# Layer 0 of two tiles at a time, full-height half chunks in attention, and loads at the turn between two phases of a four-layer net

## The chip, the cores and the metric

The kernel runs on one core of a Trainium2 chip, as one launch. The metric is the device time of one execution in microseconds (us); the number of a kernel is the median over its executions. A core has a matrix engine, TensorE (PE), whose weight loads are listed apart (PEld); three engines for elementwise work, VectorE (DVE), ScalarE (ACT) and GpSimd (POOL); and SyncE (SP), which only issues DMAs here. Each engine takes its instructions in the order of the program.

## The reference

The input x has 64 batches of 64 tokens of 512 numbers, all in float32. Four layers follow, each added to its input.

```python
x = x + (x @ W0[id] + b0[id])                  # layer 0: one of 16 matrices, chosen per batch
x = x + (x @ W1.T + ((x @ A[a].T) @ Bm[a].T) * s[a])   # layer 1: one matrix, plus a rank-16 adapter per batch
x = x + attention(x)                           # layer 2, below
x = x + (w3[sub].T @ x + b3[sub][:, None])     # layer 3: over a batch's 64 tokens, one of 8 matrices
```

Layer 2 has 8 query heads and 4 groups of keys and values of 64 numbers. Queries and keys are normalised by their root mean square, scaled by a gain and rotated by their position. New keys and values go into a paged cache at positions pos..pos+63 of each batch; a query sees the 256 positions up to its own. A softmax over these, the product with the values, and a matrix Wo end the layer.

## The kernel before, in words

The 4096 tokens are 32 tiles of 128 rows, two batches to a tile. **Phase A** (0 to about 520 us) does layers 0 and 1 and the products that make q, k and v. **Phase B** (about 520 to 954 us) does attention, layer 3 and the output, a tile per step. The program is written in the order in which every engine works (a manual schedule), so a line's place in the Python text is its place in each engine's queue, SyncE's and GpSimd's too.

*Layer 0* (`layer0`, from L243). `load_next(i)` asks SyncE for the input of tile i+2 (`load_x`, L222) and the two matrices of 1 MB that its batches use (`load_w0`, L232). Four buffers `w` exist, two tiles' worth. L249 multiplies: each matmul makes the 64 rows of one batch, so two run side by side on halves of the array's columns. ScalarE copies the result to `s0` (L252; one buffer). `add_bias` (L260, GpSimd) makes x1 = x + bias. `turn0` transposes `s0` (L273) and VectorE adds it into x1 (L274). Each matmul of the program shows as two records in the trace (L249: 8 a tile, 512 records).

*Layer 1* (`layer1`, from L612) takes a group of tiles: adapter products `pxa` (L620) and their selection `xa` (L625, VectorE), 16 matmuls a tile (L635), the adapter's second product (L643), a copy and a store of x2 (L648, L649). The groups are `GROUPS = [1, 1, 2] + [4] * 7`. After layer 1 of a group, the loop at the end of phase A (from L708) goes through the tiles of the *next* group: for each, `layer0`, `load_next`, `other`, then for one tile of the group just finished `turn_x2` (L654), the product for q (L140), `turn0` of the new tile, and the product for k and v with its normalisation and rotation: `turned` (L120 to L135), in which VectorE's L133 and L134 need the gain tiles cg and sg that GpSimd makes (L110), and GpSimd makes the sum (L135).

*`other`* feeds work in small pieces between the tiles: index and window work on VectorE (`windows`, among it `hit` and `own` at L535 and L539), rotation angles, and `old`: the copy of old cache rows. Each of 68 pieces is a GpSimd gather into a buffer `st` (L155, five buffers) and a SyncE store of 512 KB into `kvd` (L161), which is issued when three later gathers have been asked for. `other` takes pieces of `old` from tile 6 on; `layer1` takes one per tile too (from tile 4).

*The turn between the phases.* The q of the last eight tiles is left for the beginning of phase B. `parts_q` is a generator of three parts: Square, sum and Sqrt; reciprocal and scale; rotation. `turn_q` (L170 to L183) transposes (L174), ScalarE copies to `qTs` (L177; two buffers), SyncE stores to `qTd` (L181). Before the first step stand the loads of q, mask (`load_mask`) of tiles 0 and 1, `wo` and q of tile 2.

*Phase B, step s.* `load_kv(s+2)` gathers keys and values (L768, GpSimd). `scores(s)`: matmuls (L841), mask and maximum on VectorE (L849), exponential on ScalarE (L853). `attend(s-1)` multiplies probabilities by values (L888), `normalise` divides (L861, L865), `last` is layer 3 of two tiles at even steps (L928), `project(s-2)` multiplies by Wo (L916) into the one PSUM bank of the pool `pyp` and adds x2 (L920), `keys(s+1)` transposes keys (L822, L828; copies L823, L829), `turn(s)` transposes probabilities (L874, L878) into `pT` (L875 on VectorE and ScalarE, L879 on ScalarE). The queries of one batch see 320 positions: two chunks of 128 rows that belong to the batch, and a *half chunk* of 64. The half chunks of the two batches of a tile share one chunk of 128 rows: rows 0 to 63 belong to the first batch, 64 to 127 to the second. `attend` treats each with its own matmuls of 64 rows:

```python
for gp in range(2):
    for b2 in range(2):
        for g in (2 * gp, 2 * gp + 1):
            product(b2, g, slice(b2 * 64, (b2 + 1) * 64), 4, G, g, False, gp == 1)
```

PSUM has eight banks: seven in a ring that all products but one take in turn, and the one of `pyp`, which `project` uses at every step and which q of tile 31 uses at step 0.

Of the kernel before, what the change touches and what calls it, by code (L numbers as in the profile page):

```python
# [22 lines left out]
KC = D // 128  # L23
# [36 lines left out]
def body(ctx: ExitStack, tc: tile.TileContext, a: dict, out: bass.AP):  # L60
# [108 lines left out]

    def turn_q(i):  # L170
        qrf = qrs.pop(i)
        pqt = bank("pqt")
        for c in range(KC):
            TE.transpose(pqt[:, c * 128 : (c + 1) * 128], qrf[:, c * 128 : (c + 1) * 128], ident)  # L174
        qT = late.tile([128, 2, 2, 2, T], F32, name="qTs", bufs=2)
        for gp in range(2):
            S.copy(  # L177
                qT[:, gp].rearrange("p b h t -> p h b t"),
                pqt[:, gp * 256 : (gp + 1) * 256].rearrange("p (h b t) -> p h b t", h=2, b=2),
            )  # L180
        nc.sync.dma_start(  # L181
            qTd[i * 128 : (i + 1) * 128, :], qT.rearrange("p g b h t -> p (g b h t)")
        )  # L183

    with ExitStack() as pa:
# [57 lines left out]
        def layer0(i, bias=True):  # L243

            p0 = bank("p0")
            for c in range(KC):
                for h in range(2):
                    hs = slice(h * T, (h + 1) * T)
                    TE.matmul(p0[hs, :], xs[i][:, c, hs], w0s[i][h][:, c, :], start=c == 0, stop=c == KC - 1)  # L249
            w0s.pop(i)  # L250
            s0 = s0s[i] = wk.tile([128, D], F32, name="s0")
            S.copy(s0, p0)  # L252
            if bias:
                add_bias(i)
# [412 lines left out]

        biasT = su.tile([128, KC, B], F32, name="biasT")
        pb = bank("pb")
        for c in range(KC):  # L670
            TE.transpose(pb[:, c * B : (c + 1) * B], brow[:, c * 128 : (c + 1) * 128], ident[:B, :B])
        S.copy(biasT.rearrange("p c b -> p (c b)"), pb[:, : KC * B])
        layer0(0)
        turn0(0)
# [21 lines left out]
        def other(i):  # L696

            next(bg, None)
            next(bg, None)

            o = (i + 2) // 8
            if 0 < o < NT // 8 and i <= 8 * o + 2:
                next(turns.setdefault(o, rotation(o)), None)
            if i > 5:
                for _ in range(2 - i % 2):
                    next(old, None)

        for g in range(NG - 1):  # L708
# [6 lines left out]
            for k in range(m):  # L715
                i0, i = tiles[g + 1][k], tiles[g][k * n // m] if (k + 1) % (m // n) == 0 else None
                layer0(i0)
                load_next(i0)
                other(i0)
# [147 lines left out]
    def turn(i):  # L867
        pr, _ = prs.pop(i)

        pT = pTs[i] = bp.tile([128, G + 1, 512], F32, name="pT")  # L870
        for g in range(G):
# [5 lines left out]
        for g in range(G):  # L877
            TE.transpose(pt[:, g * 128 : (g + 1) * 128], pr[:, g, 256:384], ident)  # L878
        S.copy(pT[:, G, :], pt)  # L879

    def attend(i):
        kv, pT = kvs.pop(i), pTs.pop(i)
        oT = oTs[i] = bp.tile([128, KC, 2, T], F32, name="oT")
        po = [bank("po") for _ in range(2)]

        def product(b2, g, rows, n, c, m, start, stop):
            gp, g2 = divmod(g, 2)
            TE.matmul(  # L888
                po[b2][g2 * 64 : (g2 + 1) * 64, gp * 128 : (gp + 1) * 128],
                kv[rows, n, (G + g) * HD : (G + g + 1) * HD], pT[rows, c, m * 128 : (m + 1) * 128],  # L890
                start=start, stop=stop,
            )

        for b2 in range(2):
            for gp in range(2):
                for c in range(2):
                    for g in (2 * gp, 2 * gp + 1):
                        n = 2 * b2 + c

                        product(b2, g, slice(0, 128), n, g, n, gp == 0 and c == 0, False)  # L900
        for gp in range(2):
            for b2 in range(2):
                for g in (2 * gp, 2 * gp + 1):
                    product(b2, g, slice(b2 * 64, (b2 + 1) * 64), 4, G, g, False, gp == 1)
        for b2 in range(2):
            V.tensor_copy(oT[:, :, b2, :], po[b2][:, :256].rearrange("p (k t) -> p k t", t=T))

# [48 lines left out]
    for i in range(2):  # L956
        load_kv(i)
        load_q(i)
        load_mask(i)
    wo = bp.tile([128, KC, D], F32, name="wo", bufs=1)  # L960
    nc.sync.dma_start(wo, a["woT"].rearrange("(c p) f -> p c f", p=128))
    load_q(2)

    parts = {}
    for i in range(NT - LATE + 1, NT - 1):
# [3 lines left out]
        if i > NT - LATE + 2:  # L969
            turn_q(i - 2)  # L970
        if i - 1 in parts:
            run(parts.pop(i - 1))
        next(parts[i])
    keys(0)
    for s in range(NT):
        if s + 2 < NT:
# [9 lines left out]
        if s:  # L986
            load_pair(s - 1)
            attend(s - 1)
        else:

            parts[NT - 1] = parts_q(NT - 1, product(NT - 1, wq, "pq", pyp), V, cs[NT - 1])
            turn_q(NT - 3)
        normalise(s, 0)
        if s == 1:
            next(parts[NT - 1])
            next(parts[NT - 1])
        normalise(s, 1)
# [4 lines left out]
        if s + 1 < NT:  # L1002
            keys(s + 1)
        if s in (3, 4):
            turn_q(NT - 5 + s)
        turn(s)
        if s in (2, 3):
            run(parts.pop(NT - 4 + s))
    i = NT - 1
# [62 lines left out]
```

## Time and profile before

| what | value |
| --- | --- |
| median of 11 executions | 956.37 us (954.7 to 959.03) |
| the profiled execution: its own time | 956.01 us |
| its span in the profile | 953.9 us |
| its mean granted clock of TensorE | 0.995 |
| weight loads busy | 508.4 us |
| HBM read and written | 190.29 and 69.50 MB |
| L888 in all | 82.1 us in 1536 records |
| L249 in all | 121.6 us in 512 records |
| L155, gathers of old cache rows | 68, about 1.0 us each on GpSimd |

The profile is of one execution. "Busy" is the time that an engine worked, and its share of the span. A row of a group of instructions names the line, engine, operation, what it writes and reads, and how many there are. In a timeline, a row begins with its start and its duration; in brackets stands how long the engine had been idle before it and what ended that. The view of waits sums these by what was waited for. Durations of pipelined matmuls overlap a little, so what one costs is read from the start of one record to that of the next.

### The profile page before, as it was taken

The numbers are of one execution on the slowest core, as the hardware profiler recorded it, in microseconds if no ns is written. First come the engines' busy times: TensorE is split into PE (matmuls) and PEld (weight loads), VectorE is DVE, ScalarE is ACT, GpSimd is POOL, SyncE is SP. The second block draws the span as 40 slices with busy tenths as digits, with TensorE's granted clock in tenths as the row PEclk, the third lists the DMA queues.
The fourth block names the chain that finished last, engine by engine and source line by source line (L and its number), as shares of the span: only waits on it lengthen the run. The fifth ranks groups of instructions, "written<-read, shape, count | busy, mean of one in ns | idle before, by whom it ended". The sixth has DMA issues, their size and how long they took to land.

```text
span 953.9 us, 17790 instructions
## 1 busy us (share of the span) xinstructions
PE 922.5 (97%) x5397; PEld 508.4 (53%) x5397; DVE 613.9 (64%) x1736; ACT 415.0 (44%) x1084; POOL 404.9 (42%) x599
## 2 busy tenths in 40 slices
PE   4999999999999999999999799999999999999998
PEld 1344444444444444444344367666777777766665
DVE  3755998888573263532315778777777777777773
ACT  0312144221342221432213376666666666666663
POOL 3333465455353453544434454344444444444400
PEclk9999999999999999999999989999999999999999
DMA  7988999999999999999984784666666666666621
GB/s 247 354 278 274 340 363 328 385 396 332 382 340 368 397 323 394 397 340 387 398 295 178 262 255 143 216 218 193 207 201 205 202 207 203 206 208 208 206 62 46
DMA packets 133344, 260.97 MB, mean 274 GB/s; under 512 B 32737, under 2 KB 41570, under 8 KB 133250
## 3 DMA queue, kind: packets, MB, share of 16 engines
q1 hardware_dynamic: 108562, 178.61, 52.1%
q0 software_dynamic: 23280, 79.84, 25.5%
q10 hardware_dynamic: 1408, 1.39, 0.5%
q8 instruction: 43, 0.70, 0.3%
q14 instruction: 51, 0.42, 0.1%
HBM read 190.29 MB, written 69.50 MB: 272 GB/s over the span
## 4 chain that ended last, share of the span: by engine, by line
PE 69%; DMA 3%; DVE 2%; SPq 1%; ACT 1%; issue 0%; POOL 0%; ACTq 0%; DVEq 0%
PE py L916 12%; PE po L888 8%; PE ps L841 8%; PE p L635 7%; PE pk L140 7%; PE ppt L874 6%; PE p L249 6%; PE pq L140 5%; PE pkt L822 2%; PE ppt L878 2%; PE pkt L828 1%; PE pz L928 1%; DMA qTd<-qTs 1%; DMA w<-in_W 1%; PE px L654 1%; PE pqt L174 1%
## 5 line engine op out<-in xcount | busy, mean ns | idle before, releaser
L768 POOL DMA_INDIRECT kv<-kvd,idxn x128 | 126.2, 986 | 194.3 <-PE po L888 151.5
L853 ACT ACTIVATE pr<-pr,mx 128x320 f32<-128x320 f32 x256 | 140.1, 549 | 23.3 <-DVE mx L849 23.3
L849 DVE CUSTOM_DVE_ANT_0 pr<-ps,mb 128x320 f32<-128x320 f32 x256 | 107.9, 486 | 27.9 <-PE ps L841 27.5
L249 PE MATMUL p<-w,xt 128*64 128x512 f32 x512 | 121.6, 607 | 0.5 <-DMA w<-in_W 0.5
L916 PE MATMUL py<-wo,oT 128*128 128x512 f32 (+1 forms) x264 | 118.3, 591 | 0.0
L140 PE MATMUL pk<-wkv,x 128*128 128x512 f32 x256 | 115.4, 595 | 1.4 <-ACT x L656 1.4
L155 POOL DMA_INDIRECT st<-in_kvc,cidx x68 | 68.4, 1006 | 104.0 <-DMA kvd<-st 96.1
L635 PE MATMUL p<-w,x 128*128 128x512 f32 x256 | 112.5, 596 | 0.0
L140 PE MATMUL pq<-wq,x 128*128 128x512 f32 x248 | 111.3, 593 | 0.0
L841 PE MATMUL ps<-kT,qT 64*128 64x320 f32 x512 | 81.9, 454 | 5.5 <-ACT kT L823 5.3
L865 DVE TENSOR_SCALAR pr<-pr,sm 128x320 f32<-128x320 f32 x256 | 85.6, 396 | 2.2
L274 DVE TENSOR_TENSOR x<-pt,x 128x512 f32<-128x512 f32 x32 | 22.0, 688 | 98.6 <-PE pt L273 91.6
L888 PE MATMUL po<-pT,kv 128*64 128x128 f32 (+1 forms) x1536 | 82.1, 278 | 0.0
L888 PEld LDWEIGHTS po<-pT,kv 128*64 128x64 f32 (+1 forms) x1536 | 68.9, 135 | 19.8 <-DVE mx L849 13.6
L916 PEld LDWEIGHTS py<-wo,oT 128*128 128x128 f32 x264 | 47.5, 189 | 59.8 <-issue 58.6
L635 PEld LDWEIGHTS p<-w,x 128*128 128x128 f32 x256 | 47.8, 190 | 58.2 <-issue 56.5
L135 POOL TENSOR_TENSOR qr<-qn,sq 128x512 f32<-128x512 f32 x25 | 31.7, 1268 | 107.6 <-DVE qn L134 107.6
L140 PEld LDWEIGHTS pk<-wkv,x 128*128 128x128 f32 x256 | 46.3, 190 | 49.7 <-issue 47.4
L249 PEld LDWEIGHTS p<-w,xt 128*64 128x64 f32 x512 | 35.2, 138 | 70.4 <-issue 67.0
L140 PEld LDWEIGHTS pq<-wq,x 128*128 128x128 f32 x248 | 44.9, 190 | 46.2 <-issue 46.2
L133 DVE TENSOR_TENSOR sq<-qn,sg 128x256 f32<-128x256 f32 (+1 forms) x128 | 40.1, 354 | 42.2 <-POOL sg L110 40.2
L123 ACT ACTIVATE ss<-ss,epst 128x4 f32<-128x4 f32 (+1 forms) x64 | 19.2, 299 | 107.4 <-DVE ss L122 107.4
(191 smaller groups left out, 1358.3 us busy)
## 6 DMA issues: line engine op xcount, KB each, us to landing
w<-in_W SPq DMA_DIRECT2D x62, 1024.0 KB
kvd<-st SPq DMA_DIRECT2D x68, 512.0 KB
xt<-in_xT SPq DMA_DIRECT2D x32, 256.0 KB
x2d<-x2n SPq DMA_DIRECT2D x32, 256.0 KB
kvd<-kvn SPq DMA_DIRECT2D x32, 256.0 KB
qTd<-qTs SPq DMA_DIRECT2D x32, 256.0 KB
qT<-qTd SPq DMA_DIRECT2D x32, 256.0 KB
x2r<-x2d SPq DMA_DIRECT2D x32, 256.0 KB
```

What stands on the lines that cost most here:

```text
L140: TE.matmul(ps, x2s[i][:, c, :], w[:, c, :], start=c == 0, stop=c == KC - 1)
L155: P.indirect_dma_start(out=st, out_offset=None, in_=a["kvc"].rearrange("(n r) d -> n (r d)", r=2), in_offset=bass.IndirectOffsetOnAxis(ap= ...
L249: TE.matmul(p0[hs, :], xs[i][:, c, hs], w0s[i][h][:, c, :], start=c == 0, stop=c == KC - 1)
L635: TE.matmul(p1[i], x1s[i][:, c, :], w1[:, c, :], start=c == 0, stop=False)
L768: P.indirect_dma_start(out=kv[:, n, :], out_offset=None, in_=kvd, in_offset=bass.IndirectOffsetOnAxis(ap=at, axis=0),)
L841: TE.matmul(ps[g2][:, :NPOS], qT[rows, gp, b2].rearrange("p h t -> p (h t)"), kT[rows, gp, b2 * NPOS : (b2 + 1) * NPOS], start=True, stop= ...
L849: V.tensor_tensor_reduce(out=p, in0=ps[g2][:, :NPOS], in1=mb[:, b2, :], scale=-1.0, scalar=3.0e38, op0=ALU.add, op1=ALU.min, accum_out=mx[ ...
L853: S.activation(p, p, AF.Exp, bias=mx[:, g, b2 : b2 + 1], scale=-1.0, accum_out=sm[:, g, b2 : b2 + 1],)
L865: V.tensor_scalar(p, p, sm[:, g, b2 : b2 + 1], None, ALU.mult)
L874: TE.transpose(pt[:, n * 128 : (n + 1) * 128], pr[:, g, at : at + 128], ident)
L888: TE.matmul(po[b2][g2 * 64 : (g2 + 1) * 64, gp * 128 : (gp + 1) * 128], kv[rows, n, (G + g) * HD : (G + g + 1) * HD], pT[rows, c, m * 128 ...
L916: TE.matmul(py[:, fs], oT[:, c].rearrange("p b t -> p (b t)"), wo[:, c, fs], start=c == 0, stop=c == KC - 1,)
```

## The change

It has five parts. (1) Layer 0 of tile 0 stands before the transposes of the bias rows, and its `add_bias` after them. (2) In groups of four tiles, layer 0 of two tiles is done in one go at every even tile, then the loads for both next tiles; `s0` gets two buffers. (3) `other` takes pieces of `old` from tile 4 on, not from tile 6. (4) In attention the half chunks are done with matmuls of all 128 rows and both batches at once (256 columns); the probabilities lie in one of two tiles `hT`, which hold zeros where a row belongs to the other batch and are cleared once, by four memsets on VectorE ahead of phase B. Results go to one PSUM bank instead of two, and one copy takes them out instead of two. The copy of the half chunks' probabilities is split in two copies of 64 rows, one on ScalarE and one on VectorE. (5) At the beginning of phase B, q and mask of tile 1 are loaded behind the first `keys`, `wo` and q of tile 2 behind the first `turn`; `qTs` of the late tiles gets four buffers; the transposes of q of tiles 30 and 31 come a step later; and the parts of q of tiles 30 and 31 are moved to other places in steps 1 to 3.

```diff
@@ -167,12 +167,12 @@
         for _ in parts:
             pass
 
-    def turn_q(i):
+    def turn_q(i, pool=late):
         qrf = qrs.pop(i)
         pqt = bank("pqt")
         for c in range(KC):
             TE.transpose(pqt[:, c * 128 : (c + 1) * 128], qrf[:, c * 128 : (c + 1) * 128], ident)
-        qT = late.tile([128, 2, 2, 2, T], F32, name="qTs", bufs=2)
+        qT = pool.tile([128, 2, 2, 2, T], F32, name="qTs", bufs=2 if pool is late else 4)
         for gp in range(2):
             S.copy(
                 qT[:, gp].rearrange("p b h t -> p h b t"),
@@ -248,7 +248,7 @@
                     hs = slice(h * T, (h + 1) * T)
                     TE.matmul(p0[hs, :], xs[i][:, c, hs], w0s[i][h][:, c, :], start=c == 0, stop=c == KC - 1)
             w0s.pop(i)
-            s0 = s0s[i] = wk.tile([128, D], F32, name="s0")
+            s0 = s0s[i] = wk.tile([128, D], F32, name="s0", bufs=2)
             S.copy(s0, p0)
             if bias:
                 add_bias(i)
@@ -666,11 +666,12 @@
         scalars()
 
         biasT = su.tile([128, KC, B], F32, name="biasT")
+        layer0(0, False)
         pb = bank("pb")
         for c in range(KC):
             TE.transpose(pb[:, c * B : (c + 1) * B], brow[:, c * 128 : (c + 1) * 128], ident[:B, :B])
         S.copy(biasT.rearrange("p c b -> p (c b)"), pb[:, : KC * B])
-        layer0(0)
+        add_bias(0)
         turn0(0)
         load_next(0)
         load_weight(wq, "wqT")
@@ -701,7 +702,7 @@
             o = (i + 2) // 8
             if 0 < o < NT // 8 and i <= 8 * o + 2:
                 next(turns.setdefault(o, rotation(o)), None)
-            if i > 5:
+            if i > 3:
                 for _ in range(2 - i % 2):
                     next(old, None)
 
@@ -714,8 +715,15 @@
             n, m = len(tiles[g]), len(tiles[g + 1])
             for k in range(m):
                 i0, i = tiles[g + 1][k], tiles[g][k * n // m] if (k + 1) % (m // n) == 0 else None
-                layer0(i0)
-                load_next(i0)
+                if m < 4:
+                    layer0(i0)
+                    load_next(i0)
+                elif k % 2 == 0:
+
+                    for i1 in (i0, i0 + 1):
+                        layer0(i1)
+                    for i1 in (i0, i0 + 1):
+                        load_next(i1)
                 other(i0)
                 if i0 % 4 == 1 and i0 // 4 + 1 < NT // 4:
                     load_a(i0 // 4 + 1)
@@ -867,7 +875,7 @@
     def turn(i):
         pr, _ = prs.pop(i)
 
-        pT = pTs[i] = bp.tile([128, G + 1, 512], F32, name="pT")
+        pT = pTs[i] = bp.tile([128, G, 512], F32, name="pT")
         for g in range(G):
             pt = bank("ppt")
             for n, at in enumerate((0, 128, 384, 512)):
@@ -876,34 +884,37 @@
         pt = bank("ppt")
         for g in range(G):
             TE.transpose(pt[:, g * 128 : (g + 1) * 128], pr[:, g, 256:384], ident)
-        S.copy(pT[:, G, :], pt)
+
+        ht = hTs[i % 2]
+        for b2, copy in enumerate((S.copy, V.tensor_copy)):
+            hs = slice(b2 * 64, (b2 + 1) * 64)
+            copy(ht[hs, :, b2, :], pt[hs].rearrange("p (g n) -> p g n", g=G))
 
     def attend(i):
         kv, pT = kvs.pop(i), pTs.pop(i)
         oT = oTs[i] = bp.tile([128, KC, 2, T], F32, name="oT")
-        po = [bank("po") for _ in range(2)]
-
-        def product(b2, g, rows, n, c, m, start, stop):
-            gp, g2 = divmod(g, 2)
-            TE.matmul(
-                po[b2][g2 * 64 : (g2 + 1) * 64, gp * 128 : (gp + 1) * 128],
-                kv[rows, n, (G + g) * HD : (G + g + 1) * HD], pT[rows, c, m * 128 : (m + 1) * 128],
-                start=start, stop=stop,
-            )
-
+
+        po = bank("po").rearrange("p (k b n) -> p k b n", k=2, b=2)
         for b2 in range(2):
             for gp in range(2):
                 for c in range(2):
-                    for g in (2 * gp, 2 * gp + 1):
-                        n = 2 * b2 + c
-
-                        product(b2, g, slice(0, 128), n, g, n, gp == 0 and c == 0, False)
+                    for g2 in range(2):
+                        g, n = 2 * gp + g2, 2 * b2 + c
+
+                        TE.matmul(
+                            po[g2 * 64 : (g2 + 1) * 64, gp, b2], kv[:, n, (G + g) * HD : (G + g + 1) * HD],
+                            pT[:, g, n * 128 : (n + 1) * 128], start=b2 == 0 and gp == 0 and c == 0, stop=False,
+                        )
         for gp in range(2):
-            for b2 in range(2):
-                for g in (2 * gp, 2 * gp + 1):
-                    product(b2, g, slice(b2 * 64, (b2 + 1) * 64), 4, G, g, False, gp == 1)
-        for b2 in range(2):
-            V.tensor_copy(oT[:, :, b2, :], po[b2][:, :256].rearrange("p (k t) -> p k t", t=T))
+            for g2 in range(2):
+                g = 2 * gp + g2
+                TE.matmul(
+                    po[g2 * 64 : (g2 + 1) * 64, gp], kv[:, 4, (G + g) * HD : (G + g + 1) * HD],
+                    hTs[i % 2][:, g], start=False, stop=gp == 1,
+                )
+        V.tensor_copy(
+            oT.rearrange("p (k h) b t -> p k b h t", k=2), po.rearrange("p k b (h t) -> p k b h t", h=2)
+        )
 
     def project(i, ring=False, parts=1):
         py, oT = bank("py") if ring else pyp.tile([128, 512], F32, name="py"), oTs.pop(i)
@@ -955,11 +966,13 @@
 
     for i in range(2):
         load_kv(i)
-        load_q(i)
-        load_mask(i)
-    wo = bp.tile([128, KC, D], F32, name="wo", bufs=1)
-    nc.sync.dma_start(wo, a["woT"].rearrange("(c p) f -> p c f", p=128))
-    load_q(2)
+    load_q(0)
+    load_mask(0)
+
+    hTs = [bp.tile([128, G, 2, 128], F32, name=f"hT{n}", bufs=1) for n in range(2)]
+    for hT in hTs:
+        for b2 in range(2):
+            V.memset(hT[(1 - b2) * 64 : (2 - b2) * 64, :, b2, :], 0.0)
 
     parts = {}
     for i in range(NT - LATE + 1, NT - 1):
@@ -967,11 +980,14 @@
         parts[i] = parts_q(i, pq, V, cs[i])
         next(parts[i])
         if i > NT - LATE + 2:
-            turn_q(i - 2)
+            turn_q(i - 2, bp)
         if i - 1 in parts:
             run(parts.pop(i - 1))
         next(parts[i])
     keys(0)
+    load_q(1)
+    load_mask(1)
+    wo = bp.tile([128, KC, D], F32, name="wo", bufs=1)
     for s in range(NT):
         if s + 2 < NT:
             if s < 2:
@@ -989,11 +1005,10 @@
         else:
 
             parts[NT - 1] = parts_q(NT - 1, product(NT - 1, wq, "pq", pyp), V, cs[NT - 1])
-            turn_q(NT - 3)
+            turn_q(NT - 3, bp)
+        if s == 2:
+            next(parts[NT - 1])
         normalise(s, 0)
-        if s == 1:
-            next(parts[NT - 1])
-            next(parts[NT - 1])
         normalise(s, 1)
         if s % 2 == 0 and s >= 4:
             last(s - 4)
@@ -1001,11 +1016,17 @@
             project(s - 2)
         if s + 1 < NT:
             keys(s + 1)
-        if s in (3, 4):
-            turn_q(NT - 5 + s)
+        if s in (4, 5):
+            turn_q(NT - 6 + s, bp)
+        elif s in (2, 3):
+
+            run(parts.pop(NT - 4 + s))
         turn(s)
-        if s in (2, 3):
-            run(parts.pop(NT - 4 + s))
+        if s == 0:
+            load_q(2)
+            nc.sync.dma_start(wo, a["woT"].rearrange("(c p) f -> p c f", p=128))
+        elif s == 1:
+            next(parts[NT - 1])
     i = NT - 1
     load_pair(i)
     add_one(i - 1)
```

## The prediction

> **What bounds the kernel now.** I read busy time first. Columns: busy microseconds, share of the span, instructions; the two rows below give 40 slices of 23.8 us, in tenths.
>
> ```profile
> PE 922.5 (97%) x5397; PEld 508.4 (53%) x5397; DVE 613.9 (64%) x1736; ACT 415.0 (44%) x1084; POOL 404.9 (42%) x599
> ...
> PE   4999999999999999999999799999999999999998
> ...
> PEclk9999999999999999999999989999999999999999
> ```
>
> TensorE (PE) works 97% of the span. The weak slices are the first, and the 23rd (the transition to attention), where the clock row also dips. So time comes from TensorE's work, its few waits, and the clock. The view of TensorE's waits lists all the waits there are (total, times, longest):
>
> ```profile
> PE pb L671 <- DMA brow<-in_b,idcol: 11.1, 1, 11.1
> PE ps L841 <- ACT kT L823: 5.3, 1, 5.3
> PE pt L273 <- ACT s L252: 3.7, 7, 0.8
> PE pxa L620 <- DVE x L274: 2.8, 3, 1.0
> PE ppt L874 <- DVE pr L865: 2.3, 2, 2.1
> ```
>
> The profiled execution's own time is 956.01 us (span 953.9, so 2.1 around it); the median shown is 956.37. I sum against 956.0. Within 0.2%, 1.9 us, is about what a measurement of this kernel can't tell from no change.
>
> A table of busy time by stretch gives the second fact:
>
> ```profile
> 85.00:250.00 165.00, 161.06 (x634) 71.09 (x632) 143.38 (x251) 42.87 (x101) 90.11 (x126) 1.00 0.95 346
> 250.00:520.00 270.00, 268.63 (x1031) 119.60 (x1028) 110.40 (x277) 82.87 (x186) 122.58 (x224) 1.00 0.95 350
> ```
>
> The third pair is VectorE (DVE): 143 of 165 us in the first stretch, 110 of 270 in the second. In VectorE's timeline up to 233 us I found no idle but answers of 0.4 to 0.6 us from ScalarE (ACT) and GpSimd (POOL), while TensorE waits there for VectorE's x1 (1.02 at 103.14, 0.92 at 233.73). Both are at the limit there; what TensorE alone saves before 233 is taken back at the next such wait.
>
> **Start: 0 (-0.4 to +0.4).** Layer 0 of tile 0 now goes ahead of the bias transposes. TensorE waits 11.11 us for brow, and L249 runs 11.70 to 17.36, its last W0 pieces landing at 15.0. In front it could begin at 10.2, yet ends about 16.0 because of those pieces. Then pb, a copy, the bias copy, GpSimd's adds (1.65 us, now after layer 0 and not beside it), and L274 at about 18.85; it stood at 18.84.
>
> **Pairs of layer 0: -3.5 by themselves.** In single records, a matmul of L249 starts 0.429 us after the one before it; the first after a full-array one needs 0.573, and leaving for a transpose needs 0.261 where 0.109 is usual. So one block costs 0.144+0.152 = 0.296 in changes of tile shape, and a pair saves one of its two. Seven groups of four hold two pairs each. The last four groups, after 250 us, win 4x2x0.296 = 2.4, and tiles 29 to 31 lose their wait of pt for the s0 copy (0.37 each): 1.1. Of the first three groups only the first pair, ahead of VectorE's full stretch, could keep its saving (0.9: one change of shape and most of the 0.77 that pt waits at tile 4), and only if VectorE is not delayed behind it. The bounds for 3.5 are 2.4 (the waits of pt move elsewhere) and 4.4.
>
> **Three gathers moved forward: +6.7 (0 to +11).** The old cache copies start two tiles earlier. GpSimd now:
>
> ```profile
> 98.27 1.36 POOL L110 TENSOR_TENSOR cg<-gain,cos 128x64 f32<-128x64 f32 x1
> 99.59 0.31 POOL L110 TENSOR_TENSOR sg<-gsw,sin 128x64 f32<-128x64 f32 x1
> ...
> 118.36 0.94 POOL L155 DMA_INDIRECT st<-in_kvc,cidx x1 [5.62 <-DMA kvd<-st]
> ```
>
> Five st buffers exist, so the sixth gather waits for the first store of one to land: here 5.62 us at 118.36, while VectorE is occupied with `hit` work that doesn't need GpSimd. After the change the sixth gather stands in tile 7's slot, ahead of cg/sg. Its store is issued by SyncE (SP) behind the loads of w(8) and w(9), two tiles now in one go: 4.5 MB with xt. In the trace these go out at 91.6 to 95.8 and land from 97.5 to 110.8, so the store lands at about 110; then gather and gains, and VectorE's next row can start at about 111.8:
>
> ```profile
> 102.40 0.68 DVE L274 TENSOR_TENSOR x<-pt,x 128x512 f32<-128x512 f32 x1
> ...
> 105.08 0.76 DVE L133 TENSOR_TENSOR sq<-qn,sg 128x256 f32<-128x256 f32 x2
> ```
>
> 111.8-105.1 = 6.7 us of VectorE's full chain, behind which stand `xa`, the adapter work and the x1 adds that TensorE needs up to 233. Nothing is lost if the store overtakes the loads; 11 if the next odd slot also waits (the row at 118.36 was 5.6). I take 6.7, being the landing that the trace shows. Phase A: +6.7-3.5 = **+3.2**; without the stall -0.9-3.5 = -4.4.
>
> **Transition: -6.1 (-9 to -2).** ScalarE's qTs copy waits for a qTd store that stands behind q1, mask1, wo and q2 in the queue, and delays the kT copy, for which TensorE waits; a half clock follows:
>
> ```profile
> 543.21 0.65 ACT L177 COPY qTs<-pqt 128x256 f32<-128x256 f32 x2 [5.88 <-DMA qTd<-qTs]
> ```
> ```profile
> 546.38 4.64 PE L841 MATMUL ps<-kT,qT 64*128 64x320 f32 x16 [5.33 <-ACT kT L823]
> ...
> 568.40 1.93 PE L874 MATMUL ppt<-ident,pr 128*128 128x128 f32 x8 [2.05 <-DVE pr L865]
> ```
>
> With four qTs buffers and the loads behind, the wait is about 1.1: -4.2. The sixteen score matmuls need 2.4 in place of 4.64: -2.1 with the overlap. At step 1 tile 31's rotation leaves the normalises, so 2.05+0.24 go, and 3.4 us at half clock behind them: -4.0. At step 2 project(0) waits about 1.75 for the PSUM bank that q of tile 31 still holds, and parts of tile 30 stand ahead of the pT copies (0.65): +2.4, with a half clock behind a 1.75 wait, priced by its nearest row (2.05): +1.7. Steps 3 and 4: L841 took 3.31 there against 2.42; half comes back: -1.0. Four zero memsets on VectorE wait for the last kvn store (issued 520.3, landed 523.4; its SBUF region is reused) and then hold the reduction at 521.2, so tile 25's q turn: no memset of that size is in the trace; 0.06 each (a 128x1 memset, L405) to 0.69 (a 128x512 copy), taken 0.35, +1.1 at TensorE (0 to 2.5). q2 and wo, moved behind turn(0), go out at about 552 and are read at about 564 and 570; in the trace they landed 11.0 and 9.8 us after issue with 2 MB ahead of them, so they cost nothing, and a late one costs what it is late. Sum -6.1.
>
> The clock row, 0.83 for 540 to 560, shows half clock behind 5.33 and behind 2.05 us. [...]
>
> **Half chunks: +10.6 (8.5 to 12.2).** One step of attention:
>
> ```profile
> 646.51 2.42 PE L841 MATMUL ps<-kT,qT 64*128 64x320 f32 x16
> 648.86 2.56 PE L888 MATMUL po<-pT,kv 128*64 128x128 f32 x48
> 651.25 1.04 PE L928 MATMUL pz<-x,w 64*64 64x512 f32 x8
> 652.21 3.70 PE L916 MATMUL py<-wo,oT 128*128 128x512 f32 x8
> ```
>
> Of the 48 records, 16 are half chunks of 64 rows. In single records four of these start within 7 ns and a quad takes 0.109: four quads and one change of shape (0.141) make 0.598. The new form has 4 calls with 128 rows and 256 columns, eight records, of which only two run side by side: four pairs at twice 0.109 = 0.216 make 0.864 and no change of shape. +0.266 a step, 32 steps: +8.5. In the 15 even steps L928 (64x64) followed such a half chunk without a change; it now follows 128x64 records: 15x0.141 = +2.1. VectorE per step gains one pT half copy (0.69) and loses one of the two oT copies; its idle of 0.92 in front of L849 hides that. With that cover gone: 0.05 a step, 1.6 more.
>
> [...]
>
> **Sum: 956.0 + 0 + 3.2 - 6.1 + 10.6 = 963.7 us.**
>
> **Rivals.**
> - Forecast, chance 0.50, own range 959 to 969.
> - *The gather is hidden* (0.25): its store lands before 105, or VectorE has other work first. Phase A is -4.4: 956.0-4.4-6.1+10.6 = 956.1, own range 953.5 to 959. For: VectorE kept working through 118.36 now. Against: L133 waits for sg, 37 times in the trace.
> - *Transition wins in full* (0.12): faster. No half clock at step 2, no memset delay, qTs free: -9, which decides once the gather is hidden as well and the transition is under -8.1. 956.1-2.9 = 953.2, and 951.1 if L928 pays no change of shape. Against: project(0)'s bank.
> - *Loads starve* (0.13): two tiles of W0 asked for at once leave 4.5 MB in front of every store and gather; later odd slots wait too, at 11 in place of 6.7, with the transition at -2: 963.7+4.3+4.1 = 972.1. DMA share 0.95 speaks for it; TensorE's slack after 250 (VectorE 41% busy) against.
> - That the change doesn't do what it says isn't seen: instruction order on each engine moves as told.
>
> Range 952.5 to 970.0: leaves out the most of the fourth case and a half of the third. Faster by over 0.2% (under 954.5): 0.12 plus 0.05 of the second; same: 0.13 of the second and 0.02 of the forecast; slower: 0.48+0.07+0.13.
>
> **What would show it.** L888's group per step 2.83 us instead of 2.56, L928's 1.18, L906 once per step. A GpSimd gather at about 110 with a wait on kvd<-st of over 5 us, and L133 near 112. PE at the x1 wait of 233 some 6 us later. The wait for kT about 1 us. I am wrong if a step of attention grows by less than 0.2 us, if the sixth gather doesn't wait, or if the clock dip at 545 stays.

## The result, and the profile after

The changed kernel takes 1029.68 us (median of 8, 1024.8 to 1031.18) against 956.02 for the kernel before (median of 31); the ratio is 1.0761, 95% interval 1.0746 to 1.0776. The forecast was 963.7 with a range up to 970.0: the direction was right, the size wrong by a factor of ten. The profiled execution has a span of 1030.8, 76.9 more than the 953.9 of before. In some sets of runs the kernel before takes 975 to 980 us and in others 956 to 958, so a run below is compared by its ratio to the kernel before in the same set, and lengths in attention are read from sets at 956 to 958 alone.

The page of the changed kernel, busy time and the rows of TensorE (40 slices of 25.8 us):

```profile
PE 969.3 (94%) x5141; PEld 526.3 (51%) x5141; DVE 633.5 (61%) x1740; ACT 414.4 (40%) x1084; POOL 398.9 (39%) x599
...
PE   5999988997998989979989999999999999999998
...
PEclk9999989998999999999999999999999999999999
```

The weak slices are no longer two; they are spread over the whole of phase A, which is now the first 23 slices, and in two of them, the sixth and the tenth, the clock row dips to 8 tenths. TensorE is busy 46.8 us longer and idle 30.1 us longer. Its waits (total, times, longest), then those of all engines that matter:

```profile
PE pk L140 <- ACT x L656: 20.6, 13, 3.9
PE p L249 <- DMA w<-in_W: 17.3, 10, 8.6
PE pt L273 <- ACT s L252: 7.0, 6, 1.7
PE pxa L620 <- DVE x L274: 3.7, 3, 1.9
```
```profile
POOL st L155 <- DMA kvd<-st: 175.0, 23, 16.4
...
DVE sq L133 <- POOL sg L110: 121.5, 44, 14.3
```

The last two rows are the story. The same two in the kernel before:

```profile
POOL st L155 <- DMA kvd<-st: 96.1, 30, 7.2
...
DVE sq L133 <- POOL sg L110: 40.2, 37, 4.5
```

GpSimd waits 175.0 us for stores of old cache rows (96.1 before), and VectorE waits 121.5 us for the gain tiles that stand behind on GpSimd (40.2 before). The first of the changed kernel's long waits, on GpSimd and then on VectorE:

```profile
113.25 0.93 POOL L155 DMA_INDIRECT st<-in_kvc,cidx  x1 [16.37 <-DMA kvd<-st]
114.19 0.34 POOL L110 TENSOR_TENSOR cg<-gain,cos 128x64 f32<-128x64 f32 x1
```
```profile
114.83 0.76 DVE L133 TENSOR_TENSOR sq<-qn,sg 128x256 f32<-128x256 f32 x2 [9.37 <-POOL sg L110]
```

This is the sixth gather where the forecast had put it, 9.37 us of VectorE's time and not 6.7. The forecast counted it once. GpSimd's wait returns in the odd places, from the next group on (10.04 at 156.54, 9.21 at 187.93, 10.49 at 230.18), and VectorE waits 5.42, 5.10 and 7.54 us behind these three.

To say where the time went I read five marks off each trace: the end of the last group's layer 1, the first transposes of keys (L822 in the kernel before), the first `attend`, the sixth, and the length of a step as the mean of the 20 steps behind the sixth `attend`.

| trace | layer 1 ends | to keys(0) | to first attend | to the sixth | a step |
| --- | --- | --- | --- | --- | --- |
| before | 496.3 | 43.5 | 21.2 | 63.5 | 12.184 |
| after | 554.2 | 47.2 | 15.5 | 64.5 | 12.962 |
| difference | +57.9 | +3.7 | -5.7 | +1.0 | +0.778 |

From the sixth `attend` to the end of the span the changed kernel takes 20.0 us more. 57.9+3.7-5.7+1.0+20.0 = 76.9, the whole difference of the spans. So 57.9 us is phase A (61.6 up to keys(0), the figure in some of the expectations below), and about 24 (0.778 a step) is attention. Phase A loses all the way: layer 1 of tiles 12 to 15 ends at 274.3, 24.5 us late, and the other 33.4 us come after that.

### The profile page after: what moved, and what is told of

Read it like the earlier page. It is cut to its first block, busy times and chain, and to the rows that moved or that the text cites. A ratio compares the mean times of both kernels' runs of the same rounds, so it can differ in the third digit from the quotient of the medians.

```text
span 1030.8 us, 17263 instructions
## 1 busy us (share of the span) xinstructions
PE 969.3 (94%) x5141; PEld 526.3 (51%) x5141; DVE 633.5 (61%) x1740; ACT 414.4 (40%) x1084; POOL 398.9 (39%) x599
## 4 chain that ended last, share of the span: by engine, by line
PE 64%; DMA 8%; DVE 5%; ACT 2%; POOL 2%; issue 1%; SPq 0%; ACTq 0%; DVEq 0%; POOLq 0%
PE py L927 11%; PE ps L849 8%; DMA kvd<-st 7%; PE p L635 7%; PE pk L140 6%; PE po L904 6%; PE ppt L882 5%; PE pq L140 4%; PE p L249 4%; PE po L911 3%; PE pkt L830 2%; PE pz L939 1%; DMA w<-in_W 1%; PE pkt L836 1%; PE ppt L886 1%
## 5 line engine op out<-in xcount | busy, mean ns | idle before, releaser
L140 PE MATMUL pk<-wkv,x 128*128 128x512 f32 x256 | 132.8, 669 | 20.7 <-ACT x L656 20.6
L249 PE MATMUL p<-w,xt 128*64 128x512 f32 x512 | 126.8, 606 | 17.3 <-DMA w<-in_W 17.3
L155 POOL DMA_INDIRECT st<-in_kvc,cidx x68 | 66.6, 979 | 185.5 <-DMA kvd<-st 175.0
L133 DVE TENSOR_TENSOR sq<-qn,sg 128x256 f32<-128x256 f32 (+1 forms) x128 | 40.1, 355 | 123.0 <-POOL sg L110 121.5
L140 PEld LDWEIGHTS pk<-wkv,x 128*128 128x128 f32 x256 | 52.1, 213 | 82.0 <-issue 57.6
L849 PE MATMUL ps<-kT,qT 64*128 64x320 f32 x512 | 92.1, 449 | 1.5 <-issue 1.2
L249 PEld LDWEIGHTS p<-w,xt 128*64 128x64 f32 x512 | 37.8, 138 | 99.1 <-issue 76.8
L849 PEld LDWEIGHTS ps<-kT,qT 64*128 64x128 f32 x512 | 55.5, 186 | 27.4 <-issue 6.6
L904 PE MATMUL po<-pT,kv 128*64 128x128 f32 x1024 | 63.0, 276 | 0.0
```

What stands on the lines that cost most here:

```text
L140: TE.matmul(ps, x2s[i][:, c, :], w[:, c, :], start=c == 0, stop=c == KC - 1)
L155: P.indirect_dma_start(out=st, out_offset=None, in_=a["kvc"].rearrange("(n r) d -> n (r d)", r=2), in_offset=bass.IndirectOffsetOnAxis(ap= ...
L849: TE.matmul(ps[g2][:, :NPOS], qT[rows, gp, b2].rearrange("p h t -> p (h t)"), kT[rows, gp, b2 * NPOS : (b2 + 1) * NPOS], start=True, stop= ...
L904: TE.matmul(po[g2 * 64 : (g2 + 1) * 64, gp, b2], kv[:, n, (G + g) * HD : (G + g + 1) * HD], pT[:, g, n * 128 : (n + 1) * 128], start=b2 == ...
```

## The experiments

The marks of phase A are alike in all sets: layer 1 of the last group ends at 496.3 to 498.4 in seven traces of kernels that leave phase A's loop alone.

**Which part of the change costs phase A?**

b2_pair: the kernel before with the pairs alone.

```diff
-                layer0(i0)
-                load_next(i0)
+                if m < 4:
+                    layer0(i0)
+                    load_next(i0)
+                elif k % 2 == 0:
+                    for i1 in (i0, i0 + 1):
+                        layer0(i1)
+                    for i1 in (i0, i0 + 1):
+                        load_next(i1)
```

> The kernel before with part 2 alone: layer 0 of two tiles in one go, both loads behind, two s0 buffers; old cache copies from tile 6, attention and the turn between the phases as before. Theory A (pairing sets off GpSimd's waits for kvd and the chain behind them, from the second group on): about 50 us slower than before, 1000 to 1012, GpSimd's wait of st for kvd 140 us or more. Rival C (the pair needs the early start of the copies to do harm): 952 to 962.

Ratio 1.047 (1.0427 to 1.0513); layer 1 ends at 546.4, 50.1 us late; GpSimd waits 161.6 us for kvd. The pairs alone do most of the harm.

b3_i3: the early start of the old copies alone (`if i > 5` to `if i > 3`).

> The kernel before with part 3 alone: old cache copies from tile 4. My forecast's mechanism without pairs: the sixth gather, in tile 7's place, waits for the first store with the loads of one tile and not of two ahead of it, and holds the gains. The markers of c2_nopair, against those of c3_trans, give 5.4 us up to the end of the last layer 1. Expected: 958 to 963, ratio 1.003 to 1.007. Rival (hidden, as the 5.62 us wait of before was): within 0.2%.

Ratio 1.0018 (1.0005 to 1.0031). GpSimd's sixth gather does wait, 8.36 us at 105.76, but VectorE only 2.14 for the gains behind it, and layer 1 ends at 499.7, 3.4 later than in the kernel before. Part 3 alone is worth 0.1 to 0.3%, less than I expected.

c2_nopair: the changed kernel with layer 0 tile by tile; all else of the change stays.

> The changed kernel without part 2: layer 0 tile by tile, one s0 buffer; the rest of the change, the early start of the copies included, stays. Theory A: phase A is that of before within 3 us, so what is left is attention (0.778 us a step measured in the changed kernel, 32 steps, +24.5) and the turn between the phases (about -5): 956+24.5-5 = 975, range 970 to 980. Rival C (the early start by itself costs): over 985.

Layer 1 ends at 503.1, so 51.1 of the 57.9 us go with the pairs. The ratio, 1.0403 (1.0368 to 1.0438), is far over the 975 expected: this set was one of those at 979.5, where attention's new form costs more (b4_half below). In phase A 6.8 us stay, where theory A allowed 3; for the total the run tells nothing.

a2_i5: the changed kernel with old copies from tile 6.

> The changed kernel, with the old cache copies starting at tile 6 again and not at tile 4. Theory A (loads of a pair in front of the stores, at every pair): the earlier start only sets where the first wait falls; 5 to 20 us come back, 1010 to 1025. Rival C (the earlier start is the cause, as my forecast had it with one wait of 6.7 us): phase A comes back to that of before, 965 to 975.

1023.5 to 1026.4 in two runs, ratio 1.072 (1.0686 to 1.0755); GpSimd still waits 161.7 us, and layer 1 ends at 545.3, 8.9 us earlier. Rival C falls: the early start is not the cause of most of it.

**How do the pairs cost it?**

a1_spread: the pair of matmuls stays, the loads go out one tile at a time.

```diff
-                    for i1 in (i0, i0 + 1):
-                        load_next(i1)
+                if m >= 4:
+                    load_next(i0)
```

> The changed kernel, but the loads for the next two tiles no longer go out together behind a pair of layer 0: those for the first stand behind the pair, those for the second behind the next tile's place, as before the change. The matmuls stay in pairs. Theory A (the stores of old cache rows stand behind 4.5 MB of W0 at every pair; the third gather of each pair waits for one of them on GpSimd and holds the gain tiles, so VectorE, k and v, and SyncE's queue): nearly all of the 61.6 us that phase A lost comes back; time 965 to 975, GpSimd's wait of st for kvd under 110 us (it was 175.0). Rival B (two layer 0 blocks back to back starve for W0 or wait for s0): less than 20 us come back, 1010 or more.

A miss, with the time that rival B forecast: 1024.4 us, ratio 1.0715 (1.0684 to 1.0746). GpSimd's wait fell as theory A says, to 63.1 us, and VectorE's for the gains to 20.1, but layer 1 still ends at 547.7. TensorE's rows show why:

```profile
148.90 1.04 PE L249 MATMUL p<-w,xt 128*64 128x512 f32 x2 [3.11 <-DMA w<-in_W]
152.90 5.84 PE L249 MATMUL p<-w,xt 128*64 128x512 f32 x14 [2.96 <-DMA w<-in_W]
```

The second tile's matrices are now asked for a place later and behind the stores of k, v and q on SyncE, while the pair needs them a place earlier. TensorE waits 36.5 us for W0 (17.3 in the changed kernel), twice in a pair, and then runs 14 records in 5.84 us instead of 3.65. One wait was exchanged for another.

a5_ahead2: each store of old rows issued one gather earlier (`copies(kvd[:OLD], op, 3)` to `2`).

> The changed kernel, with each store of old cache rows issued one gather earlier (two gathers are asked ahead, not three), all else the same. The store on which the third gather of a pair waits then stands ahead of the pair's loads in SyncE's queue. Theory A: GpSimd's wait for kvd falls under 100 us and at least 40 of the 61.6 us come back, 965 to 990. Rival B (layer 0 pairs starve): no more than 15 us come back. Against both: SyncE may now wait for gathers to land, which would show as its own wait of L161 for st, over 60 us (25.4 now).

988.43 us, ratio 1.0338 (1.0303 to 1.0374): 41 us come back with one digit. GpSimd waits 48.2 us for kvd, layer 1 ends at 508.1. SyncE's order shows why. In the changed kernel the gather at 156.54 waits for a store that was issued at 142.12, behind the pair's loads of W0 (132.9 to 137.7); here the store for the same gather, the 13th, goes out at 122.91, ahead of those loads (129.1 to 133.3), and the gather does not wait for it.

e2_gainsfirst: the gain tiles of a place made ahead of its gathers.

```diff
+                gq = gains(0, asked[-1], late, P) if asked and i is not None else None
+                gk = gains(1, i, wk, P) if i is not None else None
                 other(i0)
```

> The changed kernel, with the gain tiles cg and sg of a place made on GpSimd ahead of the gathers; the gathers and stores stay where they are. If the gain tiles are the link between the waiting gather and VectorE: VectorE's wait of L133 for sg falls from 121.5 to under 50 us, and layer 1 of the last group ends at 515 to 535 (554.2), since the sums qr and kvn are still behind the gather. If these sums alone are the link: it ends at 545 or later, with another wait in L133's place.

993.81 us, ratio 1.0383 (1.0361 to 1.0405); layer 1 ends at 513.9, 40.3 us earlier. Here are the waits of this kernel:

```profile
POOL st L155 <- DMA kvd<-st: 145.9, 22, 15.4
```
```profile
DVE sq L133 <- POOL sg L110: 1.7, 1, 1.7
```

GpSimd waits nearly as long as ever, and it costs little, since nothing that VectorE needs at once stands behind it: a5_ahead2 and d1_gatherlast (below), each with 98 us less of this wait, end layer 1 only 5.8 and 1.5 us earlier. That is the clearest of the runs: not the wait, but what is queued behind the waiting instruction. d2_best and e1_x2early look for the cause of the 17.6 us that are left against the kernel before.

d1_gatherlast: the changed kernel with the gathers at the end of a place.

```diff
-            if i > 3:
-                for _ in range(2 - i % 2):
-                    next(old, None)
...
+                if i0 > 3:
+                    for _ in range(2 - i0 % 2):
+                        next(old, None)
```

> The changed kernel, with the gathers of old cache rows (and the stores that go with them) at the end of a tile's place in the program instead of its beginning, behind the gains and rotations of q, k and v; how many and in which tile's place is unchanged. Theory A, first form (the harm is done by what stands behind a waiting gather on GpSimd: gain tiles and sums, so VectorE, k and v): GpSimd goes on waiting for kvd, 100 us or more in all, but the layer 1 of the last group ends within 15 us of before's 496.3 (554.2 in the changed kernel), time 975 to 990. Theory A, second form (the harm is done by SyncE's queue, loads late behind stores): it ends at 530 or later, time 1005 or more.

Layer 1 ends at 512.4, 16.1 later than before: near the first form's 15 and far from the second's 530. But GpSimd's own wait fell too, to 47.7 us, where the first form had 100 or more, so this run alone would not tell the link. Its time, ratio 1.0574 (1.0546 to 1.0603), is of a set at 976 and holds attention's new form.

d2_best: parts 1, 2 and 5 in the kernel before, gathers last.

> The kernel before with parts 1, 2 and 5 of the change (layer 0 of tile 0 first, pairs of layer 0 with both loads behind, the turn between the phases), the old copies from tile 6 as before, but their gathers at the end of a tile's place; attention as before. If pairs are harmless once the gathers stand last: 945 to 955, ratio to before 0.988 to 0.999. If pairs do harm in another way: 965 or more.

Ratio 1.0126 (1.0089 to 1.0163), layer 1 ends at 514.1. The hope that pairs are harmless once the gathers stand last falls: 17.8 us of phase A stay.

e1_x2early: d2_best, with the x2 transposes and copies of both tiles in the even place.

```diff
-                if i is not None:
+                if i is not None and (m < 4 or n < 4):
                     turn_x2(i)
+                elif i is not None and k % 2 == 0:
+                    for i1 in (i, i + 1):
+                        turn_x2(i1)
```

> The kernel of the earlier run d2_best (parts 1, 2 and 5, gathers last, attention of before), and in pairs the x2 transposes and ScalarE's copies of both tiles stand in the even tile's place. With gathers last, pairs still end layer 1 of the last group at 514.1 where 496.5 is usual; TensorE waits 10.1 us for the x2 copy (L656) ahead of k and v, with half clock behind. Theory F (in an odd place there is no layer 0 block any more to cover the chain of VectorE and ScalarE of the tile before, so its x2 copy, queued on ScalarE behind that chain, comes late): the wait for L656 goes, and layer 1 ends at 500 to 506; ratio to before 0.995 to 1.003. Rival (W0 comes late): it ends at 511 or more, and L249 waits for W0 as much as before.

969.1 us, ratio 1.0121 (1.0104 to 1.0138). The wait for L656 went, from 10.1 to 1.3 us, and it brought nothing: layer 1 ends at 518.3. What binds was elsewhere, on VectorE and TensorE:

```profile
203.14 0.69 DVE L274 TENSOR_TENSOR x<-pt,x 128x512 f32<-128x512 f32 x1 [7.36 <-PE pt L273]
```
```profile
191.05 7.09 PE L249 MATMUL p<-w,xt 128*64 128x512 f32 x32
198.07 1.09 PE L654 MATMUL px<-ident,x2n 128*128 128x128 f32 x8
199.00 3.60 PE L140 MATMUL pq<-wq,x 128*128 128x512 f32 x8
202.44 0.60 PE L273 MATMUL pt<-ident,s 128*128 128x128 f32 x4
```

At the beginning of a group two blocks of layer 0 stand ahead of the first `turn0` (in this run the x2 transposes of a second tile too), so VectorE, in order and full in this stretch, waits 4.93 us in one group and 7.36 in the next (4.57 and 2.94 in d2_best, 0.2 in all before) and does not make it up: TensorE waits 4.92 us for x1 at 243.48, 9.7 us later than the kernel before did (233.73). After 250 the rest comes from W0 (waits of 3.69 and 4.09 us, with 12 records in 4.21 us behind the first and 14 in 6.06 behind the second, where 14 take 3.65 at 26.64 of the same run). Theory F named a true wait that was not the bound. What does bind is read here from the rows of one trace; no run moves the first `turn0` between the two blocks, so this part is not shown by experiment.

**What does attention's new form cost?**

a4_swap: the changed kernel, VectorE's half copy ahead of ScalarE's.

```diff
-        for b2, copy in enumerate((S.copy, V.tensor_copy)):
+        for b2, copy in ((1, V.tensor_copy), (0, S.copy)):
```

> The changed kernel, with the two copies of the half chunks' probabilities in the other order in the program: VectorE's first, ScalarE's second. In the changed kernel VectorE waits 25.0 us in 30 steps for ScalarE's copy of the same tile, then begins the masks (L857) about 0.5 us later than before, and the score matmuls take 2.85 us instead of 2.42. Theory D (this wait, not the copy itself, makes the score matmuls longer): they come back to about 2.42 to 2.5, 10 to 14 us less, 1016 to 1020. Rival E (VectorE simply has too much work per step): less than 5 us less, 1025 or more.

1019.8 us, ratio 1.0655 (1.062 to 1.0691), 10 us less. A step falls from 12.962 to 12.530. In the changed kernel VectorE's copies and the first mask of a step are:

```profile
703.72 0.69 DVE L883 COPY pT<-ppt 128x512 f32<-128x512 f32 x1 [0.18 <-issue]
705.25 0.69 DVE L891 COPY hT<-ppt 64x512 f32<-64x512 f32 x1 [0.85 <-ACT hT L891]
705.98 0.49 DVE L857 CUSTOM_DVE_ANT_0 pr<-ps,mb 128x320 f32<-128x320 f32 x1
```

The second copy waits 0.85 us for the first (25.0 us in 30 steps), although they write different rows of the tile. They also read one PSUM bank, and no run tells which of the two, tile or bank, ties them. With the copies swapped the wait does not go away: ScalarE waits 22.0 us in 32 steps for VectorE's copy instead, and there it is cheap. Here is TensorE's step in the changed kernel, then the score matmuls with the copies swapped:

```profile
678.55 2.86 PE L849 MATMUL ps<-kT,qT 64*128 64x320 f32 x16
681.34 1.97 PE L904 MATMUL po<-pT,kv 128*64 128x128 f32 x32
683.14 1.03 PE L911 MATMUL po<-hT,kv 128*64 128x256 f32 x8
684.10 1.09 PE L939 MATMUL pz<-x,w 64*64 64x512 f32 x8
685.12 3.70 PE L927 MATMUL py<-wo,oT 128*128 128x512 f32 x8
```
```profile
701.92 2.42 PE L849 MATMUL ps<-kT,qT 64*128 64x320 f32 x16
```

L904 to L939 is 2.76 us where L888 took 2.39; the score matmuls (L849), 2.86 us in the changed kernel, are back at 2.42. So 0.432 of a step's 0.778 is this wait, 0.346 the half chunks themselves.

b1_oldhalf: the changed kernel with `turn` and `attend` of before, no memsets.

> The changed kernel with attention as before (parts 1, 2, 3 and 5 stay). By the markers of the changed kernel, a step of attention costs 0.778 us more and 20 steps 15.6: about 24 us of the 73.7 are attention's, the memsets' 1 to 2 included. On a chip where the kernel before takes 956: 1004 to 1009, ratio 1.050 to 1.055. On one where it takes 976 to 980: the ratio of b2_pair (1.047) plus the early start and less the turn, 1.045 to 1.055.

1002.91 us, ratio 1.0491 (1.0433 to 1.0549), about 27 us less than the changed kernel; a step is 12.184 again.

b4_half, b4_again, b4_third: one kernel, the new attention with swapped copies in the kernel before.

> The kernel before with part 4 alone, the half chunks with 128 rows and zeros, but with VectorE's copy ahead of ScalarE's, so that VectorE does not wait for it. My forecast of the matmuls alone: +0.33 us a step, 32 steps, +10.6 and the memsets +1.1: 966 to 969. Rival E (VectorE overloaded even without the wait): 975 or more.

> The kernel before with part 4 alone and the copies swapped, once more, since on the chip of the last runs the kernel before took 979.5 us and TensorE's results were taken up later by VectorE and ScalarE in attention. On a chip where the kernel before takes about 956: +0.346 us a step as measured in the changed kernel with swapped copies, 11 to 13 in all with the memsets, 967 to 969, ratio 1.011 to 1.014. On a chip like the last one: ratio 1.03 again.

> The kernel before with part 4 alone and the copies swapped, for a chip where the kernel before takes 956: ratio 1.011 to 1.014 there; 1.03 on a chip like the last two.

Ratios 1.0325 (1.0293 to 1.0357) and 1.0339 (1.0309 to 1.0368) where the kernel before took 979.5 and 976.4, and 1.0125 (1.0108 to 1.0142) where it took 957.7: 968.57 us, a step of 12.530. The last is the price of part 4 with the copies swapped, the memsets included: 10.8 us. In the other two sets the new form costs more: its step is 13.907 and 13.848 there, and 12.7 to 12.9 with the form of before (c3 below). In the c3_third trace ScalarE's copy of pT at 701.83 begins 2.46 us after ScalarE was idle, released by a matmul of the scores that stands behind the transposes it copies (0.29 in the profile of before). That the new form leaves less slack for such a late copy is my reading; what delays the copy was not tried.

**What does the turn between the phases give?**

c3_trans, c3_again, c3_third: the kernel before with parts 1 and 5 alone.

> The kernel before with parts 1 and 5 alone: layer 0 of tile 0 ahead of the bias transposes, and the turn between the phases with its loads, buffers and q parts moved. Forecast: start 0, turn -6.1 less the memsets' +1.1, which aren't here: about -7, so 949, range 945 to 952. Rival (the turn gives nothing, since what waited for the store waits for something else): 954 or more.

> The kernel before with parts 1 and 5 alone, once more for the same reason. On a chip where the kernel before takes about 956: the turn gave 5.7 us up to the first attend and some 3 in the next five steps in the changed kernel, so 947 to 951, ratio 0.991 to 0.995. The last runs had 0.9951.

> The kernel before with parts 1 and 5 alone, the fastest so far (ratios 0.9951 and 0.9958), where VectorE and ScalarE take up TensorE's results as early as in the profile of before. By the markers of b1_oldhalf against those of before, the turn is 5.9 us shorter up to the first attend and 2.7 in the next five steps: ratio 0.990 to 0.993. If the gain depends on the chip's state, it stays at 0.995.

Ratios 0.9951 (0.9933 to 0.997), 0.9958 (0.994 to 0.9976) and 0.9963 (0.995 to 0.9977), in sets at 979.5, 976.4 and 975.6. This is the fastest version of the study, 0.4 to 0.5% faster than the kernel before. By the marks of b1_oldhalf, in a set at 957.7, the turn gives more: 43.4 to keys(0), 15.3 to the first `attend`, 60.8 to the sixth, which is 0.1+5.9+2.7 = 8.7 us less. In b1_oldhalf and e1_x2early, both in that set, the rest of the span after the sixth `attend` is 329.2, as against 329.4 before, so nothing of it is lost again there. No set at 956 came for c3 itself, so its own total there stays open.

## Why the prediction was wrong, step by step

- **Start, 0.** Right: the first x1 wait ends at 19.55, at 19.59 before.
- **Pairs of layer 0, -3.5.** Wrong, the main failure. The step charged only changes of shape and lost sight of order: "later odd slots wait too" was given 4.3 us in a rival, and slack after 250 was held against it, where in fact 33.4 of the 57.9 us were lost. The pair puts two tiles of loads ahead of the stores in every group, and alone it costs 50.1 us in phase A (b2_pair).
- **Three gathers moved forward, +6.7.** The mechanism was right, with its place (wait 16.37, release at 113.25 for "about 110", L133 at 114.83 for 112). But it was tied to the early start, which alone is worth 0.18% (b3_i3), and counted once. The wait comes from the pairs, in every group; 40.3 of the 57.9 us vanish when the gains are taken out from behind it (e2_gainsfirst). Of the 17.6 left, a5_ahead2 with its shorter waits still keeps 11.8; what makes the rest is read from rows only.
- **VectorE at its limit up to 233.** The forecast used it to cancel savings. It did not ask what a full engine in order does when its input is moved a block later: 12.3 us of VectorE's waits in e1_x2early. Its reading of VectorE's rows also passed over a sign of what was to come: behind a gather that waited 3.29 us, VectorE already waited 1.43 for the gains, and 1.16 at 208.42.

```profile
171.14 0.76 DVE L133 TENSOR_TENSOR sq<-qn,sg 128x256 f32<-128x256 f32 x2 [1.43 <-POOL sg L110]
```

- **Transition, -6.1.** Near: -8.7 by b1_oldhalf's marks, and +3.7 for the memsets to keys(0), so -5.0. The wait ahead of the first score matmuls is 1.17 us, as forecast. The memsets are the mis-sized term, +1.1 in the forecast: VectorE waits 2.45 us for the kvn store and then takes 2.37 for the four (0.485 each, with gaps of 0.14), TensorE waits 2.37 for tile 25's q, and the eight matmuls behind that wait's transposes take 4.74 us where 3.60 is usual. With the measured 0.485 in place of 0.35 for each of the four, the forecast's total is 0.5 higher.
- **Half chunks, +10.6.** The matmuls were right: 0.346 a step measured, 0.266+0.066 forecast, 10.8 us alone (b4_third). In the trace of before, each of the four matmuls of a quad starts 6 or 7 ns behind the last, 20 ns in all, and a quad takes 0.109 as forecast. The 0.598 in it does not follow from its parts (four times 0.109 and 0.141 are 0.577), which is worth 0.7 us in all. Missing was a term: "its idle of 0.92 in front of L849 hides that" held for the length of VectorE's work, not for the wait between the two copies of one tile, which added 0.432 a step: 10.8 us of the span after the sixth `attend`, and 9.9 between the two kernels' medians (a4_swap).

The forecast's rival *Loads starve*, at 972.1, named the cause of phase A's loss: loads in front of every store, and later odd slots that wait too. Its price failed, since it took one group's wait for the whole phase.

## What to carry to other kernels

When loads are moved ahead of stores in one queue, ask who waits for the stores, and what stands behind that waiter on its engine; then multiply by the number of times the loop does it. A wait alone says little: 145.9 us of it on GpSimd cost little once the gain tiles stood ahead. Two engines that copy the halves of one bank into different rows of one tile may be made to wait for each other (VectorE 25.0 us in 30 steps here), so let the busier one go first. And doing two blocks in a row can delay everyone who lives on the first: VectorE waited 4.93 and 7.36 us for its transposes in e1_x2early.

## What the runs showed of the hardware

A wait of TensorE of some 2 us is at times followed by half clock, and at times it is not. Here are the products for k and v after waits of 2.04 and 0.24 us in the changed kernel, then after 2.66 in a5_ahead2, then after 1.54 in b3_i3:

```profile
166.55 5.40 PE L140 MATMUL pk<-wkv,x 128*128 128x512 f32 x8 [2.04 <-ACT x L656]
176.93 3.70 PE L140 MATMUL pk<-wkv,x 128*128 128x512 f32 x8 [0.24 <-ACT x L656]
```
```profile
232.96 3.70 PE L140 MATMUL pk<-wkv,x 128*128 128x512 f32 x8 [2.66 <-ACT x L656]
```
```profile
153.62 5.40 PE L140 MATMUL pk<-wkv,x 128*128 128x512 f32 x8 [1.54 <-ACT x L656]
```

In the first row the granted clock is 0.67 over 166.6 to 171.8, and the slow ones among its matmuls start 0.853 us after the one before, where 0.429 is usual; in the second it is 1.00 over 176.9 to 180.6. Two waits of the same length, 2.12 us, went either way: the one ahead of 532.74 in the changed kernel is followed by 5.40 us, the one ahead of 488.36 in a5_ahead2 by 3.70. So the length of the wait alone doesn't tell here. In the first row half clock adds 1.7 us to the wait; this is a part of TensorE's longer busy time.

A memset of zeros over 64 rows by 512 numbers in fp32 took 0.485 us on VectorE, the mean of the four of the changed kernel; the forecast had taken 0.35, between two rows of the profile before.
